# Weight loads that leave out one DMA engine, for 27 chunks in place of 7

## The chip, the core and the metric

The kernel runs on one core of a Trainium2 chip. The metric is the device time of one execution in microseconds, the median of repeated runs; lower is better. Before the change it is 752.23 us (three runs, 750.66 to 753.52).

## The reference

For every pair (i, j) with i < j of 32 fields, a batch row's vector of field i is multiplied by the pair's own 128 x 128 matrix, and the result, element by element, by the vector of field j:

```python
# inputs (1024, 32, 128), W (496, 128, 128), all float32
v_i = inputs[:, I_IDX, :]
v_j = inputs[:, J_IDX, :]
transformed = jnp.einsum('bpd,ped->bpe', v_i, W)
return transformed * v_j          # (1024, 496, 128)
```

There are 496 pairs. The output has 260 MB; the weights have 32.5 MB and the inputs 16.8 MB.

## The kernel before

**Layout.** The host transposes the inputs so that one field is a tile of 128 partitions (embedding) x 1024 (batch), and orders the weights by pair. The 496 weight matrices come in 62 chunks of `WL` = 8, each a tile of 128 x 8 x 128 floats (512 KB, 4 KB in each partition). Pairs go in an order in which i falls from 30 to 0.

**Work of a pair.** A pair q is done in two halves of 512 batch columns; u = 2q + half numbers them. For the first 15 pairs `first(u)` issues one float32 matmul (line 209). For all others both operands are split into a high and a low part, and three single-pass matmuls (line 212 twice, line 221) stand for the product. ScalarE rescales the sum in between (line 213), and VectorE multiplies by field j and writes the output tile (line 227). `split_w` makes the three weight parts of two matrices at a time: line 127 on ScalarE, lines 128 to 130 on GpSimd. `split_x` does the same for a field and gives GpSimd some more work (lines 143, 144, 148).

**Stores.** An output tile `ot` holds `OG` = 4 pairs (2 MB) and is stored as a whole from ScalarE's DMA queue (line 258). There are three tiles for outputs and four more, `g0` to `g3`, that serve as output tiles until a group of four input fields is loaded into them (`load_group`, at pairs 52, 141, 219 and 313 as `XAT` says). So seven output tiles are there at the start and three from about pair 293 on. A tile can be written again only when its whole store has landed.

**Weight loads.** Raw weights go round three tiles (`WB` = 3). Chunk c is loaded in the main loop at the end of pair 8c - 16 for most chunks (`w_at`, line 179), and its first split comes about 11 pairs later. Normally `load_w` issues one transfer from SyncE (line 118). The order of all engines' instructions is the program order written in the main loop (`manual_schedule`).

**Loads apart.** For the chunks in `WAPART` the load is issued in two pieces by `load_apart`: the first `ROWS` partitions by GpSimd's software queue (line 102), the rest by SyncE (line 103). The source rows are written as `NE` blocks of 8 rows, so that the transfer falls to `NE` = 14 of the 16 DMA engines; the host permutes the rows of these chunks beforehand to match. [...]`move_on` (line 99) issues a tiny transfer into a scratch tile `mark`: `move_on(5)` once at pair 15, then `move_on(2)` three pairs after each load apart, so that a load and its step make 16, and `move_on(13)` after the last one. The loads apart are chunks 45, 47, 49, 51, 54, 58 and 60, all in the last third.

Of the kernel before, what the change touches and what calls it, by code (L numbers as in the profile page):

```python
# [11 lines left out]
P = 128  # L12
NF = 32
NQ = NF * (NF - 1) // 2
BT = 1024
# [12 lines left out]
XLEAD = 5  # L28

XG = 4  # L30
NE = 14
ROWS = 8 * NE
WAPART = (45, 47, 49, 51, 54, 58, 60)
BACK = 3
XAT = (313, 219, 141, 52)
OWAIT = 20
# [9 lines left out]
def kernel(  # L46
# [22 lines left out]
    nc = tc.nc  # L69
# [12 lines left out]
    def load_x(f, pieces=1, eng=None):  # L82
        if f == 0:

            t = rpool.tile([P, WL, P], F32, tag="w", name="x_0").rearrange("p q e -> p (q e)")
        else:
            t = xpool.tile([P, BT], F32, tag=f"x{f}", name=f"x_{f}")
        s = BT // pieces
        for k in range(pieces):
            (eng or nc.sync).dma_start(out=t[:, k * s : (k + 1) * s], in_=xt[f, :, k * s : (k + 1) * s])  # L90
        x_sb[f] = t
# [3 lines left out]
    mark = xpool.tile([32, 16], F32, tag="mark", name="mark")  # L95

    def move_on(k):

        nc.gpsimd.dma_start(out=mark[: 2 * k], in_=xt[0, : 2 * k, :16].rearrange("(b a) n -> a b n", a=k))

    def load_apart(dst, src):
        nc.gpsimd.dma_start(out=dst[:ROWS], in_=src[:ROWS].rearrange("(b a) m n -> a b m n", a=NE))
        nc.sync.dma_start(out=dst[ROWS:], in_=src[ROWS:])

    def load_group(k):
        t = xpool.tile([P, XG, BT], F32, tag=f"g{k}", name=f"x_g{k}")
        f = XG * k + 1
        nc.sync.dma_start(out=t, in_=xt[f : f + XG].rearrange("m d b -> (m d b)").rearrange("(d m b) -> d m b", m=XG, b=BT))
        for m in range(XG):
            x_sb[f + m] = t[:, m, :]  # L110

    def load_w(c, splits=(0, WL), eng=nc.sync):
        w_raw[c] = rpool.tile([P, WL, P], F32, tag="w", name=f"w_{c}")
        if c in WAPART:
            load_apart(w_raw[c], wt[c])
            return
        for a, b in zip(splits, splits[1:]):
            eng.dma_start(out=w_raw[c][:, a:b, :], in_=wt[c, :, a:b, :])
# [64 lines left out]
    w_q = {c: q for q, c in w_at.items()}  # L183
# [18 lines left out]
    def first(u):  # L202
        q, h = divmod(u, 2)
        i, c = pairs[q][0], q // WC
        r = slice(q % WC * P, (q % WC + 1) * P)
        s = slice(h * HB, (h + 1) * HB)
        po[u] = ppool.tile([P, HB], F32, tag="po", name=f"po_{u}")
        if q < nq0:
            nc.tensor.matmul(po[u], w_raw[q // WL][:, q % WL, :], x_sb[i][:, s], start=True, stop=True)  # L209
        else:  # L210
            for t in (0, 1):
                nc.tensor.matmul(po[u], w_s[c][t][:, r], x_s[i][t][:, s], start=t == 0, stop=t == 1)  # L212
            nc.scalar.mul(po[u], po[u], 1.0 + EPS)  # L213

    def second(u):
        q, h = divmod(u, 2)
        i, j = pairs[q]
        r = slice(q % WC * P, (q % WC + 1) * P)
        s = slice(h * HB, (h + 1) * HB)
        if q >= nq0:  # L220
            nc.tensor.matmul(  # L221
                po[u], w_s[q // WC][2][:, r], x_s[i][2][:, s], start=False, stop=True, skip_group_check=True
            )
        g, k = divmod(q, OG)
        if k == 0 and h == 0:
            ots[g] = out_tile(g)
        nc.vector.tensor_tensor(ots[g][:, k, s], po.pop(u), x_sb[j][:, s], ALU.mult)  # L227
        if q >= NQ - 2:
            stores.append((u + SLAG, out[g, :, k, s], ots[g][:, k, s]))
        elif g == 0 or q >= NQ - OG:  # L230
            if h == 1:
                stores.append((u + SLAG, out[g, :, k], ots[g][:, k]))
        elif k == OG - 1 and h == 1:
            stores.append((u + SLAG, out[g], ots[g]))

    for u in range(2 * NQ + LAG + SLAG):
        q = u // 2
        if u < 2 * NQ:
            i, j = pairs[q]
            if u % 2 == 0 and j == i + 1 and XG * ngroup < i - 2 - XLEAD:  # L240
                load_x(i - 2 - XLEAD)
            first(u)
            if u == 2 * nq0:
                move_on(5)
            if u % 2 == 0 and q in group_at:
                load_group(group_at[q])
            if u % 2 == 1 and q in w_at:
                load_w(w_at[q])
                if w_at[q] in WAPART:
                    back.append(q + BACK)  # L250
            if u % 2 == 0 and q in back:
                move_on(16 - NE if q < w_q[WAPART[-1]] else 13)
            if u == 2 * x_at + 1:
                load_x(0)
        if LAG <= u < 2 * NQ + LAG:
            second(u - LAG)
        while stores and stores[0][0] <= u - LAG:
            nc.scalar.dma_start(*stores.pop(0)[1:])
        if u % 2 == 1:
            ready = [t for t in todo if t[0] <= q]  # L260
            if ready:
                ready[0][2](u)
                todo.remove(ready[0])
        while later and later[0][0] <= u:
            nc.vector.tensor_tensor(*later.pop(0)[1:], ALU.subtract)  # L265
# [33 lines left out]
```

## Time and profile before

| what | value |
|---|---|
| time | 752.23 us |
| span of the profiled execution | 753.7 us |
| busy: PE, VectorE, ScalarE, GpSimd | 93%, 86%, 83%, 79% |
| bytes moved by DMA | 310.05 MB, mean 411 GB/s |
| stores of 2 MB | 122, 13.7 us from issue to landing |
| weight loads by SyncE, 512 KB | 54, 10.6 us to landing |
| weight loads by GpSimd, 448 KB | 7, 12.6 us to landing |
| steps into `mark` | 8, 0.63 us of GpSimd each |
| SyncE's remainder of a load apart, 64 KB | 7, 5.8 us to landing |

A busy share is the part of the span in which an engine worked, averaged over stages that have different limits. The page also cuts the span into 40 slices (18.8 us each) with the rate of the DMA engines in each, and names the queues: q10 carries ScalarE's transfers (the stores and four of the first input loads), q1 those of SyncE, q0 those of the software queue, and q8 and q14 fetch instructions. Where a stretch of time is shown with its figures, the columns are: start and end, its length, busy time of PE, of PE's weight loads, of VectorE, ScalarE and GpSimd (number of instructions in brackets), the granted PE clock, the busy share of the DMA engines, and the rate in GB/s.

Each transfer is worked on by up to 16 DMA engines, and the trace has a time of landing for the part of each. "Lag" below is the time from the middle one of a transfer's 16 landings to its last.

### The profile page before, as it was taken

Reading aid. Unit: us, or ns where it says so; the run is one execution under the profiler, and the core shown is the slowest. Engines: PE = TensorE matmul, PEld = TensorE weight load, DVE = VectorE, ACT = ScalarE, POOL = GpSimd, SP = SyncE. Lnnn points to the kernel's source line nnn. Section 1 sums busy time; section 2 is a strip of 40 time slices with the busy share of each in tenths; the row PEclk is TensorE's granted clock in tenths of the full one; section 3 lists DMA queues with packets and bytes.
Section 4 is the critical chain, followed back from the end, with each engine's and each line's share of the span. In section 5 each row is a group of like instructions: output and inputs, shape, how many; then the busy total and the mean of one; then the engine's idle time right before and its main releaser. Section 6 shows DMA issues by size and latency. Waiting matters only on the chain.

```text
span 753.7 us, 10976 instructions
## 1 busy us (share of the span) xinstructions
PE 702.8 (93%) x2946; PEld 553.1 (73%) x2946; DVE 651.8 (86%) x1024; ACT 625.8 (83%) x1256; POOL 591.7 (79%) x866
## 2 busy tenths in 40 slices
PE   7998999999999997988999979989999999999993
PEld 3576777778888776776787758768788777777782
DVE  3999999999998995977988869779898989788893
ACT  1298989999999987787898868889989898888892
POOL 1789999999988788486988866878888979797670
PEclk9999999999999999999999999999999999999997
DMA  9999999999999999999999997999999999999997
GB/s 344 424 428 428 401 426 425 432 425 424 428 426 430 426 426 430 403 418 423 407 432 400 414 382 310 388 431 425 423 411 426 411 429 394 427 425 425 413 418 297
DMA packets 31789, 310.05 MB, mean 411 GB/s; under 512 B 3952, under 2 KB 4080, under 8 KB 15600
## 3 DMA queue, kind: packets, MB, share of 16 engines
q10 hardware_dynamic: 19584, 261.10, 82.1%
q1 hardware_dynamic: 10880, 45.03, 15.3%
q0 software_dynamic: 1264, 3.22, 1.2%
q8 instruction: 24, 0.39, 0.2%
q14 instruction: 37, 0.30, 0.1%
HBM read 49.29 MB, written 260.05 MB: 410 GB/s over the span
## 4 chain that ended last, share of the span: by engine, by line
PE 54%; DMA 25%; POOL 10%; DVE 7%; issue 2%; ACT 1%; DVEq 0%; SPq 0%; POOLq 0%; ACTq 0%
PE po L212 34%; DMA out_dram<-ot 24%; PE po L221 16%; DVE ot L227 7%; PE po L209 3%; POOL wl L128 2%; POOL xl L143 2%; POOL wd L130 2%; POOL xd L148 2%; POOL xl L144 1%; DMA x<-in_xt_dram 1%; POOL wd L129 1%; DVE xd L265 1%; ACT wh L127 0%; ACT po L213 0%
## 5 line engine op out<-in xcount | busy, mean ns | idle before, releaser
L213 ACT ACTIVATE po<-po 128x512 f32<-128x512 f32 x962 | 544.8, 583 | 93.5 <-PE po L212 51.8
L227 DVE TENSOR_TENSOR ot<-po,x 128x512 f32<-128x512 f32 x720 | 457.6, 684 | 70.1 <-DMA out_dram<-ot 33.6
L212 PE MATMUL po<-xh,wh 128*128 128x512 f32 x962 | 380.1, 395 | 20.8 <-DVE ot L227 20.1
L212 PE MATMUL po<-xl,wl 128*128 128x512 f32 x962 | 378.1, 393 | 11.7 <-POOL wl L128 10.4
L221 PE MATMUL po<-xd,wd 128*128 128x512 f32 x962 | 376.2, 391 | 1.8 <-DVE xd L265 0.9
L128 POOL TENSOR_TENSOR wl<-w,wh 128x256 fp32r<-128x256 f32 x241 | 182.5, 757 | 80.4 <-ACT wh L127 76.4
L212 PEld LDWEIGHTS po<-xh,wh 128*128 128x128 f32 x962 | 181.5, 189 | 71.1 <-DVE ot L227 33.1
L212 PEld LDWEIGHTS po<-xl,wl 128*128 128x128 f32 x962 | 181.7, 189 | 54.3 <-POOL wl L128 16.1
L221 PEld LDWEIGHTS po<-xd,wd 128*128 128x128 f32 x962 | 181.4, 189 | 41.1 <-ACT po L213 2.4
L130 POOL TENSOR_TENSOR wd<-wl,wd 128x256 fp32r<-128x256 f32 x241 | 178.6, 741 | 20.1
L227 DVE TENSOR_TENSOR ot<-po,x_g 128x512 f32<-128x512 f32 x272 | 171.4, 685 | 20.8 <-DMA out_dram<-ot 11.7
L129 POOL TENSOR_SCALAR wd<-wh 128x256 fp32r<-128x256 f32 x241 | 100.3, 416 | 20.4
L127 ACT ACTIVATE wh<-w 128x256 fp32r<-128x256 f32 x241 | 99.3, 413 | 7.2 <-DVE ot L227 7.2
L143 POOL TENSOR_TENSOR xl<-x_g,xh 128x512 fp32r<-128x512 f32 x32 | 41.5, 1296 | 0.0
L143 POOL TENSOR_TENSOR xl<-x,xh 128x512 fp32r<-128x512 f32 x20 | 26.3, 1314 | 15.7 <-ACT xh L142 15.4
L144 POOL TENSOR_SCALAR xl<-xl 128x512 fp32r<-128x512 f32 x52 | 34.9, 670 | 4.6
L209 PE MATMUL po<-x,w 128*128 128x512 f32 x60 | 30.3, 664 | 4.0 <-DMA x<-in_xt_dram 3.9
L265 DVE TENSOR_TENSOR xd<-xh,xl 128x512 fp32r<-128x512 f32 x32 | 29.5, 922 | 0.0
L209 PEld LDWEIGHTS po<-x,w 128*128 128x128 f32 x60 | 12.3, 211 | 21.2 <-issue 14.1
L148 POOL TENSOR_TENSOR xd<-xh,xl 128x512 fp32r<-128x512 f32 x20 | 25.8, 1292 | 1.7
L142 ACT ACTIVATE xh<-x 128x512 fp32r<-128x512 f32 x20 | 12.4, 627 | 11.4 <-DMA x<-in_xt_dram 11.2
L142 ACT ACTIVATE xh<-x_g 128x512 fp32r<-128x512 f32 x32 | 20.2, 630 | 0.0
(7 smaller groups left out, 11.2 us busy)
## 6 DMA issues: line engine op xcount, KB each, us to landing
out_dram<-ot ACTq DMA_DIRECT2D x122, 2048.0 KB, 13.7
w<-in_wt_dram SPq DMA_DIRECT2D x54, 512.0 KB, 10.6
x_g<-in_xt_dram SPq DMA_DIRECT2D x4, 2048.0 KB, 18.5
x<-in_xt_dram SPq DMA_DIRECT2D x14, 512.0 KB, 9.7
w<-in_wt_dram POOLq DMA_DIRECT2D x7, 448.0 KB, 12.6
out_dram<-ot ACTq DMA_DIRECT2D x6, 512.0 KB, 9.4
x<-in_xt_dram ACTq DMA_DIRECT2D x4, 256.0 KB, 5.7
out_dram<-ot ACTq DMA_DIRECT2D x4, 256.0 KB, 8.4
```

Source lines behind the costliest of these rows:

```text
L127: nc.scalar.mul(h, raw, 1.0 - 2.0**-13)
L128: nc.gpsimd.tensor_tensor(l, raw, h.bitcast(F32), ALU.subtract)
L129: nc.gpsimd.tensor_scalar(d, h.bitcast(F32), EPS, 1.0, ALU.mult, ALU.mult)
L130: nc.gpsimd.tensor_tensor(d, l.bitcast(F32), d.bitcast(F32), ALU.subtract)
L143: nc.gpsimd.tensor_tensor(l, x_sb[f][:, s], h.bitcast(F32), ALU.subtract)
L144: nc.gpsimd.tensor_scalar(l, l.bitcast(F32), 1.0 / EPS, 1.0, ALU.mult, ALU.mult)
L148: nc.gpsimd.tensor_tensor(d, h.bitcast(F32), l.bitcast(F32), ALU.subtract)
L209: nc.tensor.matmul(po[u], w_raw[q // WL][:, q % WL, :], x_sb[i][:, s], start=True, stop=True)
L212: nc.tensor.matmul(po[u], w_s[c][t][:, r], x_s[i][t][:, s], start=t == 0, stop=t == 1)
L213: nc.scalar.mul(po[u], po[u], 1.0 + EPS)
L221: nc.tensor.matmul(po[u], w_s[q // WC][2][:, r], x_s[i][2][:, s], start=False, stop=True, skip_group_check=True)
L227: nc.vector.tensor_tensor(ots[g][:, k, s], po.pop(u), x_sb[j][:, s], ALU.mult)
```

## The change

Loads apart are used for every second chunk from 8 to 60, 27 in place of 7. `NE` becomes 15, so a load apart covers 120 partitions and leaves out one DMA engine in place of two; the remaining 8 partitions go by SyncE as before. The step after a load now has to make up 1 engine in place of 2. It is written as a copy of 17 rows (32 - 15), and the last one as a copy of 24 rows in 12 blocks. With the first step of 5 unchanged, the engine left out is meant to be the same for all 27 loads, the fifth of the ring. The aim is to take weight traffic off one DMA engine that has other work to do, over nearly the whole run.

```diff
-NE = 14
+NE = 15
 ROWS = 8 * NE
-WAPART = (45, 47, 49, 51, 54, 58, 60)
+WAPART = tuple(range(8, 62, 2))
...
     def move_on(k):
-        nc.gpsimd.dma_start(out=mark[: 2 * k], in_=xt[0, : 2 * k, :16].rearrange("(b a) n -> a b n", a=k))
+        n = k if k > 16 else 2 * k
+        nc.gpsimd.dma_start(out=mark[:n], in_=xt[0, :n, :16].rearrange("(b a) n -> a b n", a=k))
...
             if u % 2 == 0 and q in back:
-                move_on(16 - NE if q < w_q[WAPART[-1]] else 13)
+                move_on(32 - NE if q < w_q[WAPART[-1]] else 12)
```

The other edits rewrite the load of an input group and the host's loop over these groups in more lines, with the same effect.

More of the change, by code (lines that the diff above doesn't have):

```diff
@@ L107, in load_group @@
         f = XG * k + 1
-        nc.sync.dma_start(out=t, in_=xt[f : f + XG].rearrange("m d b -> (m d b)").rearrange("(d m b) -> d m b", m=XG, b=BT))
+        rows = xt[f : f + XG].rearrange("m d b -> (m d b)").rearrange("(d m b) -> d m b", m=XG, b=BT)
+        nc.sync.dma_start(out=t, in_=rows)
         for m in range(XG):
@@ L278 @@
     xt = _np.ascontiguousarray(x.transpose(1, 2, 0))
-    for f in range(1, XG * 4, XG):
-        xt[f : f + XG] = xt[f : f + XG].transpose(1, 0, 2).copy().reshape(XG, P, BT)
+    for k in range(4):
+        f = XG * k + 1
+        some = xt[f : f + XG].transpose(1, 0, 2).copy()
+        xt[f : f + XG] = some.reshape(XG, P, BT)
     wt = _np.ascontiguousarray(w[perm].reshape(NQ // WL, WL, P, P).transpose(0, 3, 1, 2))
```

## The prediction

> **What bounds the kernel now.** I read the page's engine and DMA lines first, then the chain, then the waits, then the trace by stretches of time.
>
> ```profile
> DMA  9999999999999999999999997999999999999997
> GB/s 344 424 428 428 401 426 425 432 425 424 428 426 430 426 426 430 403 418 423 407 432 400 414 382 310 388 431 425 423 411 426 411 429 394 427 425 425 413 418 297
> ...
> q10 hardware_dynamic: 19584, 261.10, 82.1%
> q1 hardware_dynamic: 10880, 45.03, 15.3%
> q0 software_dynamic: 1264, 3.22, 1.2%
> q8 instruction: 24, 0.39, 0.2%
> ```
>
> The DMA engines are the bound: the five queue shares add up to 98.9% of 16 engines' span, and undisturbed slices move 424 to 432 GB/s. 310.05 MB at 428 GB/s is 724 us, and head and tail of the span lose about 10 more. PE's 93% is no rival: it is a busy share with waits inside the pipeline, and the chain of waits shows stores under it:
>
> ```profile
> PE 54%; DMA 25%; POOL 10%; DVE 7%; issue 2%; ACT 1%; DVEq 0%; SPq 0%; POOLq 0%; ACTq 0%
> PE po L212 34%; DMA out_dram<-ot 24%; PE po L221 16%; DVE ot L227 7%; PE po L209 3%; POOL wl L128 2%; POOL xl L143 2%; POOL wd L130 2%; POOL xd L148 2%; POOL xl L144 1%; DMA x<-in_xt_dram 1%; POOL wd L129 1%; DVE xd L265 1%; ACT wh L127 0%; ACT po L213 0%
> ```
>
> The waits say that the product at line 227 waits 45.3 us for stores, 32 times, the longest 7.1 us. By stretches (last three columns: PE clock, DMA share, GB/s):
>
> ```profile
> 220.00:300.00 80.00, 76.01 (x327) 60.38 (x326) 67.79 (x111) 70.42 (x144) 67.27 (x100) 1.00 1.01 428
> 300.00:450.00 150.00, 135.00 (x576) 108.27 (x576) 121.72 (x196) 123.99 (x248) 115.36 (x170) 0.98 1.00 415
> 450.00:460.00 10.00, 9.88 (x32) 7.93 (x33) 8.69 (x15) 6.11 (x12) 2.63 (x4) 0.72 0.39 164
> 460.00:480.00 20.00, 18.84 (x84) 15.27 (x83) 18.57 (x28) 17.79 (x37) 17.82 (x26) 1.00 0.99 377
> 480.00:527.00 47.00, 44.50 (x192) 35.48 (x191) 38.62 (x64) 40.83 (x83) 37.41 (x56) 1.00 1.01 428
> ```
>
> DMA is full to 300 us, loses rate from 300 to 480, and at 450 stands mostly empty. Why, the landings of the 16 parts of each transfer tell: in the stores the last part comes 0.8 us after the middle one at 41 us, 3.4 at 160, 5.7 at 204, 8.6 at 293 and 8 to 10 from 343 to 450, while the second last stays within 2.9 almost everywhere. **One engine of 16 falls behind**, and a store frees its tile only when that engine is done. The page names the extra load: queue q8, instruction fetches, 24 packets of 16 KB that take 0.96 us each in the trace. Seven fall between 53 and 204 us: 6.7 us, about the lag grown by then. Once the lag exceeds what the output tiles can hold (fewer towards the end: `XAT` takes them for x), the product waits (7.1 us ending at 449) and the 15 other engines run dry. From 528 us on, where the seven loads apart lie, the lag stays at 1.6 to 3.4.
>
> [...] No run here shows the 17-row step. [...]
>
> **The change part by part.**
>
> *Relief.* A load of 512 KB gives each engine 8 packets of 4 KB. Apart, engine 4 gets none of the 120 rows[...]; a 4 KB packet takes 0.155 us in a full stream (start to start). So it is relieved of 8 x 0.155 = 1.2 us against the other 15, less the 17 short rows (the old step's 2 rows of 64 B took 13 ns, so about 0.1 us): 1.1 us per load, every 16 pairs, about 24 us. The fetches cost it 0.96 us per 30 us, or 0.77 per 24. The relief covers the lag with something over. I take the lag as gone from 80 us on; the fourth engine, no longer spared, had no lag of its own worth naming (the second last landing above).
>
> *What that gives back.* Loss of a stretch = length x (428 - rate)/428. 300-450: 150 x 13/428 = 4.6; 450-460: 10 x 264/428 = 6.2; 460-480: 20 x 51/428 = 2.4; together 13.1 us. Undisturbed stretches lose 0.2% too, 0.4 us, so **12.7 us** can come back. The loads from 528 on are already relieved; there I expect nothing.
>
> *Cost of the software queue in DMA rate.* The seven old loads apart fall into these stretches:
>
> ```profile
> 551.00:565.00 14.00, 14.00 (x64) 11.58 (x63) 13.06 (x21) 12.92 (x27) 12.30 (x21) 1.00 1.01 408
> 572.00:582.00 10.00, 10.00 (x46) 8.28 (x45) 9.04 (x16) 9.68 (x22) 8.78 (x13) 1.00 1.01 422
> 632.00:645.00 13.00, 13.00 (x59) 10.74 (x58) 11.63 (x19) 12.11 (x25) 11.47 (x19) 1.00 1.01 390
> ...
> 645.00:676.00 31.00, 29.71 (x129) 23.58 (x128) 26.52 (x43) 27.48 (x56) 25.50 (x38) 1.00 1.01 427
> ```
>
> With the four not shown (527-538 at 413, 595-607 at 398, 676-689 at 420, 699-710 at 401) they lose 0.14 to 1.15 us each, 4.1 in all, mean 0.59; the stretches between, with hardware loads, lose 0.3 us in 99. So a load apart has a price: its packets stretch each other and the stores. Twenty more loads (27 for 7) cost 20 x 0.14 = 3 to 20 x 1.15 = 23 us. Eighteen of the 27 lie ahead of 480 us, where 4 to 7 output tiles keep more stores queued and engines less in step than the 3 tiles behind it; I take **0.35** there (between the lowest and the mean), and the mean for the other two: 18 x 0.35 + 2 x 0.59 = **7.5 us**.
>
> *GpSimd.* Twenty loads at 0.62 us and 20 steps at 0.63, some 0.1 between: about 29 us more on an engine busy for 592 of 754. Queued behind each are the splits at lines 128 to 130, and behind them PE. From 90 to 220 us GpSimd is 92% busy and the chain runs through it, so the splits will come later there, by perhaps 5 us in all. That is hidden as long as stores are queued, which the full DMA row shows; I cost it at nothing, with 5 as the other end.
>
> *Arrival.* Loads by GpSimd are issued at their place in its order, not as soon as the tile is free. First use is 11 pairs later, at 1.4 us a pair 15 us; the old ones land in 10.1 to 13.1, and no wait of line 127 for them exists. Hidden, with 2 us to spare. The remainder by SP lands in 5.8.
>
> *Steps and rewritten lines.* The x group load and its host loop are the same work: nothing.
>
> Sum: 752.2 - 12.7 + 7.5 = **747.0 us**.
>
> **The rivals.** (1) *A transfer price that eats the gain*: at the mean of 0.59 for all 20, 752.2 - 12.7 + 11.8 = 751.3, no change. For it: the mean is measured, and the cause of the stretching may not care for tiles in reserve. (2) *The price at its upper end*: 1.15 for all 20 gives 762.5, slower. Against: only one of seven was so dear. (3) [...]the spared engine wanders, the lag stays and reaches into the last 200 us; 752.2 + 11.8 and 3.2% of 200 us is 770. (4) *GpSimd becomes the bound*, or loads come late: if 5 us of splits and 0.5 us for each of 27 loads reach the end, 747.0 + 18.5 = 765.5, slower.
>
> **How the numbers follow.** Forecast with its neighbourhood (price 0.1 to 0.4) 0.52; rival 1 0.28; rivals 2, 3 and 4 together 0.20. Of the first nearly all lies below 748.4, of rival 1 a little, of both a part between 748.4 and 756: faster 0.54, same 0.27, slower 0.19. The low end is the lowest price with a tail 1 or 2 us shorter: 752.2 - 12.7 + 2.8 - 1.8, about 740; the high end leaves out half of the last group: 759.
>
> **What will show it.** Right: the last landing of a store no more than 3 us behind the middle one from 100 to 480 us, no hole at the old 450, waits for stores well below 45.3 us, q0 near 13 MB. The price is right if stretches with a load apart before 480 us lose about a third of a us. Wrong: a lag that still grows (rival 3), line 127 waiting for w (rival 4), slices below 410 GB/s along the whole span (rivals 1 and 2).

## The result: slower, 763.26 us

The changed kernel takes 763.26 us (four runs, 762.6 to 764.21) against 751.44 of the kernel before, run beside it: a ratio of 1.0154, 95% interval 1.0127 to 1.0181. The forecast was 747.0, with a range up to 759. Line numbers of the changed kernel are 2 higher than before from the middle of the helpers on: the splits on GpSimd are 130 to 132, the product 229, ScalarE's first split 129.

The DMA lines and two of the queues on the page after:

```profile
DMA  9999999999999999999999988999999999999998
GB/s 346 425 426 432 425 429 431 408 378 398 428 428 425 424 422 428 414 423 420 405 415 417 428 339 333 379 431 408 417 421 426 398 420 389 427 380 385 407 428 341
...
q1 hardware_dynamic: 8208, 34.97, 11.8%
q0 software_dynamic: 4784, 13.31, 5.1%
```

The bytes moved as planned: q0 has 13.31 MB. But the hole near 450 us (slices 24 to 26) is still there, there is a new one near 150 to 190 us (slices 8 to 10: 408, 378, 398) and another near 670 us (slices 36 and 37: 380, 385).

The chain of waits, by engine, and three rows of the waits after (total us, times, longest):

```profile
PE 66%; DMA 16%; POOL 9%; DVE 5%; issue 2%; ACT 1%; DVEq 0%; ACTq 0%; SPq 0%; POOLq 0%
```

```profile
DVE ot L229 <- DMA out_dram<-ot: 33.8, 21, 7.5
...
PE po L214 <- POOL wl L130: 20.3, 16, 2.1
...
ACT wh L129 <- DMA w<-in_wt_dram: 7.7, 2, 6.2
```

The waits for stores fell from 45.3 us to 33.8, but the longest is as long as before (7.5, before 7.1). PE's waits for GpSimd's split doubled from 10.4. And ScalarE waits for a weight load, a row that was not there at all.

Two measures serve all runs below. The *loss* of a stretch is as in the prediction, length x (428 - rate)/428, summed over 10 us pieces of the profiled execution. The *lag* is the median, over all transfers with 16 landings whose middle one falls into 40 us, of the time from this middle one to the last.

| loss in us | 80-220 | 220-300 | 300-450 | 450-480 | 480-530 | 530-720 |
|---|---|---|---|---|---|---|
| before | 1.6 | 0.1 | 4.6 | 8.6 | 0.0 | 4.4 |
| after | 4.4 | 0.5 | 4.7 | 8.2 | 1.5 | 9.5 |
| no loads apart (e2) | 1.8 | 0.2 | 4.5 | 7.0 | 0.0 | 5.4 |
| GpSimd dummies only (e10) | 6.3 | 0.0 | 2.5 | 7.6 | 0.2 | 4.8 |
| 34-row step (e5) | 6.4 | 0.7 | 2.3 | 2.9 | 1.3 | 10.3 |
| 34 rows, no chunk 56 (e6) | 8.1 | 0.7 | 2.3 | 1.9 | 2.8 | 5.0 |
| 34 rows, from chunk 22 (e9) | 0.8 | 0.5 | 3.8 | 2.5 | 3.0 | 5.2 |
| 34 rows, mixed list (e14) | 0.1 | 0.6 | 4.8 | 4.5 | 0.7 | 4.3 |

| lag in us | 160-200 | 280-320 | 400-440 |
|---|---|---|---|
| before | 4.0 | 7.8 | 9.4 |
| after | 2.8 | 5.6 | 8.2 |
| no loads apart (e2) | 4.3 | 7.7 | 9.3 |
| 34-row step (e5) | 1.5 | 2.4 | 3.7 |
| 34 rows, index 12 left out (e7) | 2.2 | 5.6 | 7.7 |
| 17 rows, from chunk 22 (e12) | 5.4 | 8.8 | 8.3 |

Single profiled executions lie up to some 3 us from the median of their kernel: those of e5, e6 and e9 are the fastest of their runs (e5: 757.29 us, the median 760.01), the one of e1 is the slowest. So the tables show where time goes, and the medians how much.

### The profile page after: what moved, and what is told of

Same layout as the page of the kernel before. It is cut to its first block, busy times and chain, and to the rows that moved or that the text cites. A ratio compares the mean times of both kernels' runs of the same rounds, so it can differ in the third digit from the quotient of the medians.

```text
span 760.8 us, 11073 instructions
## 1 busy us (share of the span) xinstructions
PE 701.8 (92%) x2946; PEld 555.3 (73%) x2946; DVE 671.5 (88%) x1024; ACT 625.6 (82%) x1256; POOL 615.4 (81%) x906
## 3 DMA queue, kind: packets, MB, share of 16 engines
q0 software_dynamic: 4784, 13.31, 5.1%
## 4 chain that ended last, share of the span: by engine, by line
PE 66%; DMA 16%; POOL 9%; DVE 5%; issue 2%; ACT 1%; DVEq 0%; ACTq 0%; SPq 0%; POOLq 0%
PE po L214 41%; PE po L223 20%; DMA out_dram<-ot 12%; DVE ot L229 4%; PE po L211 4%; DMA x<-in_xt_dram 3%; POOL xl L145 2%; POOL wl L130 2%; DMA w<-in_wt_dram 2%; POOL xd L150 2%; POOL xl L146 1%; POOL wd L132 1%; DVE xd L267 1%; POOL wd L131 1%; ACT po L215 0%
## 5 line engine op out<-in xcount | busy, mean ns | idle before, releaser
L229 DVE TENSOR_TENSOR ot<-po,x 128x512 f32<-128x512 f32 x720 | 469.2, 687 | 54.4 <-DMA out_dram<-ot 26.8
L130 POOL TENSOR_TENSOR wl<-w,wh 128x256 fp32r<-128x256 f32 x241 | 180.6, 750 | 64.3 <-ACT wh L129 60.0
L223 PEld LDWEIGHTS po<-xd,wd 128*128 128x128 f32 x962 | 182.2, 189 | 45.3 <-issue 4.7
L229 DVE TENSOR_TENSOR ot<-po,x_g 128x512 f32<-128x512 f32 x272 | 177.1, 688 | 25.3 <-PE po L223 15.2
L211 PE MATMUL po<-x,w 128*128 128x512 f32 x60 | 28.3, 628 | 3.8 <-DMA x<-in_xt_dram 3.8
```

The source lines that it names most:

```text
L130: nc.gpsimd.tensor_tensor(l, raw, h.bitcast(F32), ALU.subtract)
L223: nc.tensor.matmul(po[u], w_s[q // WC][2][:, r], x_s[i][2][:, s], start=False, stop=True, skip_group_check=True)
```

## The experiments

Kernels with the label e1 to e4 ran together, then e5 to e8, e9 to e12, and e13 with e14; each group had runs of the kernel before on its chip (752.78, 753.05, 752.32 and 752.97 us).

### Chunk 56 (e1)

```diff
-WAPART = tuple(range(8, 62, 2))
+WAPART = tuple(c for c in range(8, 62, 2) if c != 56)
```

> Loads apart for every second chunk from 8 to 60 but without chunk 56, which is issued only 6 pairs ahead of its first split (its due time, line 179, leaves out the usual 6 early pairs for chunks 55 to 57); all others have 11. Theory A (late arrival): the wait of line 129 for w of 6.2 us at 671 us goes, the hole in the DMA rate at 670 to 690 us (3.4 us lost) fills, and the time falls from 763.3 to about 759. Rival (the software queue's price is what counts, and the hole only moves to the next load): 762 or more, with other waits of equal size.

Measured: 761.91 us, ratio 1.0128 (1.0096 to 1.0161), an interval that overlaps that of the changed kernel. The wait of 6.2 us is gone and the loss from 530 to 720 us is 6.9 in place of 9.5, but the loss from 80 to 220 is larger (7.0). The time is nearly the rival's 762 and decides nothing at this noise; e6 below repeats the edit where it can be seen. What the wait was is plain from the timelines of ScalarE and GpSimd in the changed kernel (start, length, instruction, and in brackets the idle time before and its cause):

```profile
669.62 1.81 ACT L215 ACTIVATE po<-po 128x512 f32<-128x512 f32 x3
677.65 0.42 ACT L129 ACTIVATE wh<-w 128x256 fp32r<-128x256 f32 x1 [6.22 <-DMA w<-in_wt_dram]
```

```profile
665.83 0.67 POOL L103 DMA_DIRECT2D w<-in_wt_dram  x1
```

The load is issued at 665.8, and ScalarE wants it at 671.4, 5.6 us later; it comes at 677.6. Behind that split on ScalarE stand the rescalings of line 215, and behind them PE.

### No loads apart (e2), and the software queue over all engines (e3, e13)

e2 sets `WAPART = ()` and has no steps. e3 is the changed kernel with `NE = 16`, no remainder and no steps; e13 is e3 without chunk 56.

> No loads apart at all: all 62 weight chunks go by SyncE over 16 engines, no steps. The unrelieved engine then falls behind in the last third too. Theory A (the lag costs as much as I said, about 3% of the last 200 us): about 757, with store lags of 6 us and more after 540 us. Rival (the software queue's price in the kernel before, 4.1 us, is as large as what its seven loads give): 748 to 753, so leaving engines out hardly pays at any time.

Measured: 754.82 us, ratio 1.0038 (1.0025 to 1.0052). The old seven loads were worth 2 us, not 5 and not nothing: between the two theories. The lag after 540 us was 4.6, not 6.

> The same 27 chunks by the software queue, but over all 16 engines: no engine is left out, no remainder by SyncE, no steps. Against the kernel without loads apart it shows the software queue alone. Theory A (each load apart has a price of its own, mean 0.59 us, for what the software queue does to the stream): 27 x 0.59 = 16 us slower than without loads apart, and the dips in the rate stay. Rival (the price comes from leaving an engine out, from the remainder or from the steps): within 4 us of the kernel without loads apart, dips gone.

Measured: 758.17 us, 1.0087 (1.0058 to 1.0116), 3.4 above e2 where a price of 0.59 asked for 16. The rival's number held. Its picture did not quite: dips are still there (loss 9.7 from 530 to 720), though nothing was left out.

> 26 chunks by the software queue over all 16 engines, no steps, nothing left out, without chunk 56. It carries the software queue's transfers and half of the GpSimd time of the change, and nothing else of it. If each load apart had the price I took in the prediction (0.35 to 0.59 us): 9 to 15 us above the kernel without loads apart, 764 or more. If the price is nearly nothing, and the 3.4 us by which the 27 chunks over 16 engines lay above that kernel are GpSimd's time and chunk 56: 754 to 756.

Measured: 756.36 us, 1.0058 (1.0041 to 1.0075), 1.5 above e2. So by the medians **26 loads by the software queue cost 0.06 us each**, GpSimd's time for them (0.59 us each) included; from the lower end of e2's interval to the upper end of this one it is 3.8 us, or 0.14 each. Chunk 56 was then 1.8 of the 3.4, again with intervals that overlap; e3 has a wait of 6.0 us for that load, and e13 none. The loss from 530 to 720 us is 6.4, and e2, with no load apart, has 5.4 there. Without chunk 56 in the list, the last third loses 4 to 7 us in every kernel; when some loads go by the software queue, the dips gather at those. In e2 the seven stretches where the old loads apart lie lose 2.0 us and the stretches between them 2.8; in the kernel before it is 4.1 and 0.3.

### Which engine is left out (e4, e8, e5, e7)

> The changed kernel with its first step 13 in place of 5 (last one 4 in place of 12), so that the engine left out is index 12 instead of 4. Theory A (index 4 is the engine that fetches instructions, and relief of just this one holds the lag at 1 to 3 us up to 240 us): here the lag reaches 6 us by 200 us, and the time is 5 us or more above the changed kernel's 763.3. Rival (which engine is left out makes no difference, the lag from 240 us on has another cause): 763 within 2, with the same lags.

The edit: first step 13 in place of 5, last 4 in place of 12. Measured: 761.03 us, 1.012 (1.0094 to 1.0147), lag 4.0 at 160 to 200 us. Theory A asked for 5 us more than 763.3, and it was not slower at all; only the early lag is nearer to this theory (2.8 in the changed kernel). So the engine left out may not be what the code says, and the packets of the steps show why. Each 17-row step leaves nine packets with data in q0, eight of 128 bytes (two rows) and one of 68, that start almost together, for example at 96.54, 96.55, 96.58, 96.61, 96.62, 96.65, 96.97, 97.00 and 97.94 us, and beside them seven of 8 bytes: 16 in all, as many as a step has landings (16 more packets of 4 bytes, which each step has too, are left out). So nine of the 16 parts had rows, and I take a part for an engine; the trace doesn't name the engine. The other steps show how this is counted: they have as many packets of 128 bytes as `move_on` is given, 5, 2 and 13 in the kernel before, and the rest to 16 has 8 bytes.

```diff
-mark = xpool.tile([32, 16], F32, tag="mark", name="mark")
+mark = xpool.tile([34, 16], F32, tag="mark", name="mark")
...
-        n = k if k > 16 else 2 * k
+        n = 2 * k
```

> The changed kernel with a step of 34 rows in place of 17 (2 rows for each of 17 blocks, as all other steps have; the scratch tile gets 34 partitions). In the changed kernel a step's packets start nine at a time, within 0.2 to 2 us, two rows in each: nine engines, so the step may not move the queue's starting engine by one. [...] Theory B (the engine left out wandered; with a right step it is always the same one, the fetching one): the steps' packets come from one engine, the lag of stores stays below 4 us from 100 to 450 us, the hole at 450 us goes, and the time is 746 to 752 (the kernel over 16 engines by the software queue, 758.2, less up to 12 us). Rival C (leaving out engines costs as much as it gives, wherever it is): 758 or more.

Measured: 760.01 us, 1.0093 (1.0076 to 1.011). Now each step has one packet of 2176 bytes, which is all 34 rows, beside 15 of 136 bytes. The lag stays below 4 us to 440 us, and the hole at 450 is nearly filled (before, 450 to 460: 164 GB/s):

```profile
450.00:460.00 10.00, 9.46 (x43) 7.50 (x42) 8.48 (x15) 8.27 (x17) 5.61 (x9) 1.00 0.93 395
```

The lag is as theory B says, and its time wrong: 8 us come back between 300 and 480, and the kernel is still slower than before. One thing besides the aim has changed with it: a 34-row step holds GpSimd for 0.95 us, a 17-row step for 0.61, which makes 9 us more of GpSimd over 26 steps. How much that costs is not shown.

> The kernel with 34 rows, but first step 13 and last 4, so that index 12 is left out, always. Theory B: the fetching engine now carries its share of loads that 15 engines take; lag above 6 us by 200 us, 8 us from 260 on, time 10 us or more above the kernel with 34 rows and index 4 left out, about 760 or more. Rival C: as the kernel with 34 rows within 2 us.

Measured: 766.29 us, 1.0177 (1.0162 to 1.0192), 6.3 above e5, with the lag at 5.6 and 7.7 again. With the 34-row step the index left out matters, and of the two tried 4 is the one that holds the lag (2.4 and 3.7 in e5). The lag at 200 us was lower than I expected, perhaps because the stream was slower there (below), and the difference of 6 less than the 10 I had asked for.

> The changed kernel with no step after its loads (the one at pair 15 stays)[...]. If the 17-row step doesn't move the starting engine at all (theory B in its simplest form), this is the changed kernel less 27 small copies: 760 to 763, with the same lags. Rival: the 17-row step moves it by 1 as meant, or by 9; then times or lags differ from the changed kernel's, by more than 3 us or 3 us of lag between 100 and 240 us.

The edit drops the two lines that call for the step. Measured: 760.39 us, 1.0096 (1.0081 to 1.0111). The time is inside the first expectation; the lag at 200 to 240 us (4.4 against 1.3) is 3.1 off where the rival asked for more than 3. This speaks for the rival, a step that moves the starting engine, but barely, and does not show how far. The kernel is 2.9 us faster without its 27 steps by the medians, and 4.4 by the ratios to the kernel before; which engines are left out without the steps is not shown, so this need not be the price of the steps alone.

### Chunk 56 again (e6)

> The same with chunk 56 loaded by SyncE again. Theory B with the late arrival of chunk 56 still a cost (1.4 us where it was tried alone): 1 to 4 us below the kernel with 34 rows. Rival: the same within 1 us.

Measured: 755.45 us, 1.0039 (1.002 to 1.0058), 4.6 below e5, a little more than expected. The stretch of the late load, from 670 to 690 us, in the changed kernel and then in this one:

```profile
670.00:690.00 20.00, 15.17 (x59) 11.74 (x58) 13.81 (x22) 11.99 (x25) 15.04 (x24) 0.91 0.92 353
```

```profile
670.00:690.00 20.00, 20.00 (x90) 16.57 (x89) 17.77 (x28) 18.53 (x37) 17.62 (x29) 1.00 1.01 422
```

PE does 90 matmuls there in place of 59.

### GpSimd's time (e9, e10, e11)

e9 and e11 have the 34-row step, no chunk 56, and start at chunk 22 and at 30. e10 is e2 with three GpSimd operations for each chunk of the list in the places of the load and its step:

```diff
+        nc.gpsimd.tensor_scalar(mark, x_sb[NF - 1][:, :256], EPS, 1.0, ALU.mult, ALU.mult)
```

> No loads apart and no steps, but 81 dummy operations on GpSimd (scaling 128 x 256 of a field into a scratch tile, 0.41 us each), two at the place of each of the 27 loads and one three pairs later: GpSimd's time of the change without its transfers. Theory D: the loss of DMA rate from 80 to 220 us rises from 1.8 to 5 us or more, dips at 130 to 190 us appear; the time rises from 754.8 by less than that, since the later waits for stores shrink. Rival (the dips are made by the software queue's packets): loss and time as without loads apart, within 1.5 us.

Measured: 756.58 us, 1.0061 (1.0039 to 1.0083), 1.8 above e2; the intervals overlap, though the fastest run (756.19) is slower than the slowest of e2 (755.93). The loss from 80 to 220 us is 6.3 against 1.8, without a single transfer of the change. From 80 to 130 and 130 to 180 us, in e2 and then in e10 (columns as before; read the number of matmuls and the last column):

```profile
80.00:130.00 50.00, 47.46 (x206) 38.02 (x205) 49.72 (x77) 45.06 (x92) 46.14 (x64) 1.00 1.01 419
130.00:180.00 50.00, 49.20 (x216) 39.97 (x215) 50.00 (x78) 46.94 (x96) 46.06 (x66) 1.00 1.01 425
```

```profile
80.00:130.00 50.00, 44.15 (x189) 34.94 (x189) 46.60 (x71) 41.59 (x85) 45.66 (x66) 1.00 1.01 427
130.00:180.00 50.00, 47.87 (x203) 38.80 (x202) 47.01 (x72) 44.08 (x91) 44.89 (x68) 0.97 0.96 387
```

GpSimd is as busy in both, 46 of 50 us: it had no more room in e2 already. So what is put on it comes out of the splits, PE does 189 matmuls in place of 206, stores come too slowly, and 50 us later the DMA rate drops (387 GB/s in place of 425). The end moves by 1.8 us only, as theory D said: part of the loss is made up later (from 300 to 450 us 2.5 us are lost in place of 4.5). With the true transfers the same stretches look alike (e5):

```profile
80.00:130.00 50.00, 44.41 (x189) 35.15 (x190) 47.44 (x72) 41.85 (x85) 46.36 (x64) 1.00 1.01 425
130.00:180.00 50.00, 47.34 (x207) 38.52 (x207) 50.00 (x73) 45.15 (x93) 46.28 (x66) 1.00 1.00 396
```

> 34-row step, every second chunk from 22 on but without 56 (19 loads): the seven loads of 80 to 250 us, where GpSimd is busy 92% before any change and the DMA rate fell to 392-396 GB/s at 130-180 us, go back to SyncE. Theory D (GpSimd's 1.2 us for each load and step makes it the bound there and starves the DMA queues; the lag is worth 8 us later): the loss of 6 to 8 us from 80 to 220 us goes back to 1.6, the lag is 5 us at 220 us and then falls, time 747 to 750, faster than before. Rival E (each load apart has a price wherever it is, and the gain at 450 us only came because compute was already behind): 753 or more.

Measured: 751.99 us, 0.9997 (0.9979 to 1.0015): 3.5 below e6, since the loss from 80 to 220 us is 0.8 again, but not faster than the kernel before. The time given was too low by 2 to 5 us. 3.0 us are now lost from 480 to 530, where nothing was. The long wait for a store, which ended at 449 us, now ends at 482, after the last field group has taken its tile (its load is issued at 466): the waits for stores from 480 to 535 us are 7.1 us, the longest 5.6, and before they were 3.4, the longest 2.0. That the field group is the cause is not shown.

> As the run from chunk 22, but from chunk 30 on (15 loads, the first at about 320 us). Theory D: the lag is already 8 us when relief begins and shrinks by only 0.3 us a load, so the hole at 450 us stays in part: 750 to 753. Rival E (price per load): four loads fewer than from 22 make it 1.5 us faster than that.

Measured: 750.25 us, 0.9981 (0.9966 to 0.9996). The time is theory D's and, as far as medians tell, the rival's too; its interval touches that of e9. The loss from 450 to 480 is 2.6, but from 300 to 450 it is 6.7, where the kernel before has 4.6: the hole has moved forward, and the two stretches lose 9.3 together in place of 13.2. Inconclusive.

### Does the place of the relief matter in the better list (e12)

> The list from chunk 22 with the 17-row step of the changed kernel, so that the engine left out wanders. Theory D: lag of 8 us at 300 to 450 us as without relief, the hole at 450 us stays (6 us lost from 450 to 480), time 754 to 758. Rival (where the relief goes makes no difference in this list): as the run from 22 with 34 rows, within 1.5 us.

Measured: 758.28 us, 1.0083 (1.0057 to 1.0108), 6.3 above e9, which has the same list and the 34-row step. The lag is 8.8 and 8.3, and 8.9 us are lost from 450 to 480. Theory D, and the plainest comparison of all: the two kernels differ in nothing but the step, and the shorter step is the slower one.

### Joined with the old list (e14)

```diff
+WAPART = tuple(range(22, 44, 2)) + (45, 47, 49, 51, 54, 58, 60)
```

> 34-row step, engine 4 left out for chunks 22 to 42 (even ones) and then for the seven chunks of the kernel before. It joins relief of the middle third to the late list. Theory D: the holes of 300 to 480 us are half filled and the last third is as before: 747 to 750, below the kernel before. Rival: the stalls move to the places where output tiles go to x (as the 5.6 us wait near 515 us in the run from 22), 751 to 753.

Measured: 749.69 us, 0.9963 (0.9949 to 0.9976), 3 us faster than the kernel before. The hole from 300 to 480 is filled by a third (9.3 us lost in place of 13.2), not by half, and the last third is as it was. The wait of e9 that this expectation puts near 515 us ends at 482.

## Why the prediction was wrong, step by step

**What bounds the kernel: right.** One DMA engine falls behind (9.4 us at 400 to 440 us) and stores wait for it (45.3 us of waits). With index 4 left out the hole at 450 us is nearly filled (e5, 395 GB/s in place of 164); with index 12 left out the lag stays at 7.7 and the time is 6.3 us longer (e7). The forecast's count of the fetches was off: five of q8's 24 fall between 53 and 204 us, not seven. Five make 4.8 us, which fits the lag better (0.8 to 5.7 us). That they run on the engine behind is inferred from this sum and from e5 and e7; the trace doesn't name the engine of a packet.

**Relief: wrong, and this was the first step to fail.** The forecast takes a step of 17 rows for one engine, so that the engine left out stays the same. That was my assumption; no run had shown it. The 17 rows went in nine packets, two rows in each of eight and one in the last. It seems, then, that the engine left out was not always the one behind: of the 12.7 us 0.3 came back (300 to 480 us lose 12.9 in place of 13.2); with the same list and one packet with all rows in each step 6.3 us come back (e9 against e12, with lags of 8.8 and 8.3 us in e12). Such a failure was rival 3, within 0.20 for rivals 2, 3 and 4. Which engine a load leaves out after a 17-row step stays open.

**What it gives back: mis-sized.** The loss was summed rightly (13.1 us), but a right step brings back 8 to 9 of it (300 to 480 us, e5 and e6), not 12.7, and even e5 and e6 are slower than the kernel before. So a right step alone would not have made the forecast come true; the two terms below that stood at nothing are needed as well.

**The price of the software queue: mis-sized.** I took 7.5 us for 20 more loads, with 3 to 23 as bounds. By the medians it is 1.5 for 26 (e13), which is less than my lower end. The dips lie at the loads apart, and I took place for cause. What was missing is the loss of the last third without such loads; e2 has it, 5.4 us against 4.4. In the trace of the kernel before, a 16 KB packet of a store takes 622 to 659 ns on average in the seven stretches with a load apart and 613 to 615 in the six between, so packets do stretch there; that the loads' packets are the cause, as the forecast says, no run shows. e13 has `NE = 16`; a price of 15 engines and a remainder was not measured apart.

**GpSimd: costed at nothing, wrongly.** "That is hidden as long as stores are queued, which the full DMA row shows." A full row doesn't show how long the queue is. The rate fell 50 us later (387 GB/s from 130 to 180 us), and the loss from 80 to 220 us rose by 4.5 us in e10. My other end, 5 us, had the size of the loss in that stretch; its worth at the end is 1.8 us in e10, with intervals that overlap, and 3.5 for the early loads with their steps (e9 against e6), with intervals that don't.

**Arrival: wrong for one chunk of 27.** "First use is 11 pairs later" comes from line 179, and the same line exempts chunks 55 to 57: chunk 56 has 6. The old list leaves these three out. It costs 4.6 us where it is clear of noise (e5 against e6), and 1.4 and 1.8 by medians alone (e1; e3 against e13).

**Sum.** From the kernel without loads apart (754.8): the software queue 1.5 (e13), chunk 56 1.8 (e3), leaving out engines without a step between the loads, with SyncE's remainders, 2.2 (e8 against e3), the steps 2.9 (the changed kernel against e8): 763.2. Each term is the difference of two neighbours in a row of kernels, so that the sum comes out by itself and proves nothing. The kernels ran on different chips, and by the ratios to the kernel before, run beside each, the terms are 1.5, 2.2, 0.7 and 4.4. Against the kernel before there are 2 us more, since its seven loads with their steps were worth that (e2). Of the rivals, 3 (wandering) and 4 (GpSimd and lateness) came true together, each smaller than its number (770 and 765.5); I had treated them as alternatives to the forecast, and ended the range below both.

## What to carry to other kernels

Where a scheme rests on which engines a transfer uses, count the packets of one such transfer in a trace before summing anything: nine packets with data where one was meant left 0.3 of 12.7 us. GpSimd, busy 92% in a stretch, had no room there, whatever bounded the kernel as a whole: with more to do it stayed at 46 of 50 us, and PE did 189 matmuls in place of 206 (e10). The full DMA row hid this delay for about 50 us only (427 GB/s, then 387). And a dip in a rate beside a new kind of transfer is not its price until a like stretch without it has been looked at.

## What the runs showed of the hardware

A 17-row copy of 64 bytes a row on the software queue went in nine packets with rows, eight of two rows and one of one row (the changed kernel); 34 rows, given as 17 blocks of two, went in one packet of 2176 bytes (e5). A 512 KB load by the software queue cost about 0.06 us beyond one by SyncE (e13 against e2, 0.14 at the ends of the intervals). A load of 448 to 512 KB took 0.59 to 0.67 us of GpSimd, a 17-row step of 1.1 KB 0.61 and a 34-row step of 2.1 KB 0.95, so the time did not go by bytes. One DMA engine of 16 fell behind, by 9.4 us at 400 to 440 us (before); leaving index 4 out of every second weight load held the lag within 4 (e5, to 440 us), and leaving out index 12 did not (e7, 7.7).
